# A fused Perceiver layer: late matmuls ahead of the fourth transposes, the time-step projection in the products' second bank, and the joining of blocks in three steps

## The chip, the cores and the metric

The kernel runs on one NeuronCore of one Trainium2 chip. The metric is the device time of one execution in microseconds (us), and a time is the median of several executions. A profile is one execution, recorded by the hardware profiler. The engines are PE (TensorE, matrix products; its weight loads are listed as PEld), DVE (VectorE), ACT (ScalarE), POOL (GpSimd) and SP (SyncE, which issues most transfers). Each engine works through its own queue in program order, and waits where an operand or a buffer is not ready.

## The reference

The layer has three parts, each added to a residual stream `x` of 16 sequences with 128 rows of 512 numbers, all in fp32. First comes cross-attention, 16 heads of 32, over a context of 2048 rows per sequence. Then a state-space (Mamba) block with 1024 channels and 16 states, followed by an MLP with norms. The last part is a small mixture of experts. What matters here is the first two:

```python
def _L0_xattn_ref(queries, context, wq, bq, wk, bk, wv, bv, wo, bo):
    q = queries @ wq.T + bq
    k = context @ wk.T + bk
    v = context @ wv.T + bv
    ...
    attn = jnp.einsum('bhnd,bhsd->bhns', q, k) * scale
    attn = jax.nn.softmax(attn, axis=-1)
    out = jnp.einsum('bhns,bhsd->bhnd', attn, v)
    ...
    return out @ wo.T + bo

def _mamba(Z, in_proj_w, conv_w, conv_b, x_proj_w, dt_proj_w, dt_proj_b, A_log, D, out_proj_w):
    xz = jnp.einsum('bld,ed->ble', Z, in_proj_w)
    x, z = jnp.split(xz, 2, axis=-1)
    x = jax.nn.silu(_causal_dw_conv(x, conv_w, conv_b))
    x_dbl = jnp.einsum('bld,ed->ble', x, x_proj_w)
    dt, Bm, Cm = jnp.split(x_dbl, [DTR, DTR + DS], axis=-1)
    dt = jax.nn.softplus(jnp.einsum('blr,dr->bld', dt, dt_proj_w) + dt_proj_b)
    ...
    y = ys.transpose(1, 0, 2) + x * D
    y = y * jax.nn.silu(z)
    return jnp.einsum('bld,ed->ble', y, out_proj_w)
```

## The kernel before, in words

**Steps.** One loop (L1152) runs over 314 steps `u`. In the first 256, a step does one block of attention: one sequence `b`, one quarter `sb` of its context (512 rows), one group `hg` of four heads. So 4 steps make a quarter and 16 a sequence. Work of other stages is hung into the same steps: each step reads what the dictionaries `loads`, `middle`, `late`, `after` and `inner` hold for it (L1058 to L1112). The order is written out by hand; no scheduler moves anything. What is called `late` is matmul work of other stages: the normalized inputs turned (`turned`) and projected to queries (`queries`), the rescaling of a sequence's four quarters (`scaled`, twice in each of two steps), the output projection (`attended`), the transposes for the state-space block (`z_turned`), its input projections (`x_part`, `z_part`), `x_proj`, the time-step projection (`dt_first`) and the output projection (`projected`).

**A step of attention**, in the order of TensorE's queue: `scores` (L299) of four heads into the four PSUM banks `banks[0..3]`; `weighted` (L343), which is the product with `v` of the step before, into `avp`; `x_products` (L237), two products for the next context block, into `pa` and `pc`; four `turn`s (L330), each of which transposes a quarter of the exponentials into one bank; the late matmuls, in banks 0, 1, 2 of the step; and `y_products` (L237). In odd steps the last is one product into `pa`, in even steps two, into `pc` and `pa`.

**Who empties the banks.** VectorE takes the row maxima of the scores (L307), ScalarE the exponentials (L317). The transposes of turns 0, 1 and 3 are copied out by ScalarE (L335), those of turn 2 by VectorE (L333). Late results are read by ScalarE or VectorE, as the stage needs. A bank's next writer on TensorE waits until it has been read.

**Joining.** Each quarter has its own row maxima. When a sequence is done, `joined` (L418 to L424, VectorE) gathers them and takes their differences to the common one, `shares` (L428, ScalarE) takes exponentials, and `joined_last` (L433 to L436, VectorE) makes the factors that `scaled` applies. They stand in the steps `e`, `e + 1` and `e + 1` after the sequence's last, `e` being a multiple of 16.

**The state-space block** lags behind, for two sequences at a time (a group, 32 steps). Per step, `decays` (L653, ScalarE) and `scan` (L667, L670, VectorE) are done twice, with the products before on GpSimd (L632) and the sums after (L683). `dt_first` (L599 to L608) is a small matmul, read from its bank by ScalarE (Abs, L603) and VectorE (L606). It is due at `s - 3 + 4 * ec`, which leaves 3 when divided by 4. The gate silu(z) is `silu_first` (L551 to L553, three ScalarE operations, in `after`), `silu_second` (L558, VectorE, at the step's end) and `silu_third` (L562, L563, ScalarE and GpSimd, in the next step). `Z_GATES` holds the steps, counted from the group's start, at which the eight channel blocks are due.

**After step 255** the attention's banks serve the MLP and the experts, whose matmuls are fed into the remaining 58 steps of the scan.

Of the kernel before, what the change touches and what calls it, by code (L numbers as in the profile page):

```python
# [34 lines left out]
def perceiver_layer(ctx: ExitStack, tc: tile.TileContext, a: dict, out: bass.AP):  # L35
# [68 lines left out]
    NG = B // GB  # L104
    NU = B * SB * 4
    LAG = 22
    Z_GATES = (20, 22, 23, 24, 25, 36, 38, 40)
    NF = B // MB
    with ExitStack() as es:
        acon = es.enter_context(tc.tile_pool(name="acon", bufs=1))  # L110
# [18 lines left out]
        pc = psum.tile([P, 2, 256], FP, tag="pc", name="pc")  # L129
# [11 lines left out]
        def heads(ps):  # L141
            return ps.rearrange("p (k q) -> p k q", q=P)
# [137 lines left out]
        def x_sums(of, g, ph, pa, pc):  # L280
            sums[of](g, ph, ph, pc, held[of])
# [41 lines left out]
                )  # L323
            prs[u] = pr

        def turn(u, i):

            ps = heads(banks[i])
            for j in range(4):
                nc.tensor.transpose(ps[:, j, :], prs[u][:, j, i * P : (i + 1) * P], ident)  # L330
            pT = pool.tile([P, 4, P], FP, tag="pT", name="pT", bufs=4)
            if i == 2:
                nc.vector.tensor_copy(pT, ps)  # L333
            else:
                nc.scalar.copy(pT, ps)  # L335
            pts[u, i] = pT
# [76 lines left out]
        def joined(b):  # L413

            parts, sm = stats[b]
            nm = keep.tile([P, SB, H], FP, tag="nm", name=f"nm{b}")
            for j in range(4):
                nc.vector.tensor_copy(  # L418
                    nm.rearrange("p s (k j) -> p s k j", j=4)[:, :, :, j], parts[j]
                )  # L420
            lo = keep.tile([P, 1, H], FP, tag="lo", name="lo")
            flat = lo.rearrange("p a h -> p (a h)")
            nc.vector.tensor_reduce(flat, nm.rearrange("p s h -> p h s"), AX.X, ALU.min)
            nc.vector.tensor_tensor(nm, lo.to_broadcast([P, SB, H]), nm, ALU.subtract)  # L424
            stats[b] = nm, sm, lo, flat

        def shares(b):
            nc.scalar.activation(stats[b][0], stats[b][0], AF.Exp)  # L428

        def joined_last(b):  # L430
            nm, sm, lo, flat = stats[b]
            stats[b] = nm
            nc.vector.tensor_tensor(sm, sm, nm, ALU.mult)  # L433
            nc.vector.tensor_reduce(flat, sm.rearrange("p s h -> p h s"), AX.X, ALU.add)
            nc.vector.reciprocal(lo, lo)
            nc.vector.tensor_tensor(nm, nm, lo.to_broadcast([P, SB, H]), ALU.mult)  # L436

        fxs = {}
# [300 lines left out]
        def load_wex():  # L739
            fcs["wex"] = fpool[0].tile([P, KC, D], FP, tag="wex", name="wex")  # L740
            nc.sync.dma_start(fcs["wex"], a["wex"])
# [313 lines left out]
            units[-1][1].extend([call(experts, m, i), call(gated, m, (i,)), call(result, m, i)])  # L1055


        late, after, inner, middle, loads = ({} for _ in range(5))  # L1058

        def put(where, u, f):  # L1060
            where.setdefault(u, []).append(f)

        for b in range(B):
            s = 16 * b
            if b:
                put(loads, s - 8, lambda b=b: load_x(b))
                put(loads, s - 5, lambda b=b: load_w(0, b))
                put(inner, s - 7, lambda b=b: moments_of(b))
                put(middle, s - 6, lambda b=b: root_of(b))
                put(inner, s - 6, lambda b=b: normal(b))  # L1070
                put(late, s - 5, lambda ps, b=b: turned(b, ps))
                put(late, s - 4, lambda ps, b=b: queries(b, ps))
            e = s + 16
            put(loads, e + 5, lambda b=b: load_w(3, b))
            put(inner, e, lambda b=b: joined(b))
            put(middle, e + 1, lambda b=b: shares(b))
            put(inner, e + 1, lambda b=b: joined_last(b))
            for sb in range(SB):
                put(inner, e + 2 + sb // 2, lambda b=b, sb=sb: spread_out(b, sb))
                put(late, e + 3 + sb // 2, lambda ps, b=b, sb=sb: scaled(b, sb, ps))  # L1080
            put(late, e + 6, lambda ps, b=b: attended(b, ps))
            put(middle, e + 7, lambda b=b: root_of(b))
            put(inner, e + 7, lambda b=b: normed(b))
            put(late, e + 8, lambda ps, b=b: z_turned(b, ps))
        for g in range(NG):
            p = 32 * (g + 1)
            for ec in range(EC):
                put(loads, p + 8 + ec, lambda g=g, ec=ec: load_win(g, ec))
                put(loads, p + 8 + ec, lambda g=g, ec=ec: load_win(g, EC + ec))
                put(late, p + 9 + ec, lambda ps, g=g, ec=ec: x_part(g, ec, ps))  # L1090
                put(late, p + 9 + ec, lambda ps, g=g, ec=ec: z_part(g, ec, ps))
                put(after, p + 10 + ec, lambda g=g, ec=ec: silu_first(g, ec, xas))
                put(after, p + Z_GATES[ec], lambda g=g, ec=ec: silu_first(g, ec, zss))
            put(late, p + 18, lambda ps, g=g: x_proj(g, ps))
            s = p + LAG
            for ec in range(EC):
                put(loads, s - 4 + 4 * ec, lambda ec=ec: load_dtproj(ec))
                put(late, s - 3 + 4 * ec, lambda ps, g=g, ec=ec: dt_first(g, ec, ps))
                put(middle, s - 2 + 4 * ec, lambda g=g, ec=ec: dt_second(g, ec))
                put(inner, s - 2 + 4 * ec, lambda g=g, ec=ec: dt_third(g, ec))  # L1100
            for i in range(GB):
                for ec in range(WS):
                    put(loads, s + 32 + 2 * i, lambda g=g, i=i, ec=ec: load_wout(g, i, ec))
                put(loads, s + 31 + 2 * i, lambda b=g * GB + i: reload_x(b))
                put(late, s + 33 + 2 * i, lambda ps, g=g, i=i: projected(g, i, ps))
# [32 lines left out]
        ps = banks[2]  # L1138
# [13 lines left out]
        for u in range(last):  # L1152
            live = u < NU
            g, r = divmod(u - 32 - LAG, 32)
            scans = 0 <= g < NG

            made, phase = divmod(u + 3, 4)
            makes = 0 < made < B * SB
            of, phase = ("k", "v")[phase // 2], phase % 2
            load_bc(u + 2 - 32 - LAG, 0)  # L1160
            if u % 4 == 1 and made + 1 < B * SB:
                load_ctx(made + 1, ("c00", "c10", "c11"))
            if u % 4 == 2 and made + 1 < B * SB:
                load_ctx(made + 1, ("c01",))
            for f in loads.get(u, ()):
                f()
            if scans:
                decays(g, r, 0)
            if u > NU:
                while fed < feeds * (u - NU) // (last - 1 - NU):  # L1170
                    feed(fed)
                    fed += 1
            load_bc(u + 1 - 32 - LAG, DS)
            if u == NU + 1:
                load_rows()
            if live:
                scores(u)
            if 1 <= u <= NU:
                weighted(u - 1)
            if u == NU:  # L1180
                att.close()
                open_ffn()
            if u == NU + 8:
                load_wex()
            if live:
                maxima(u)
            if makes:
                x_products(of, made, phase, pa, pc)
            if live:
                exps(u)  # L1190
            if makes and u % 4 == 1:
                ctx_sums(made, ("t1", "t2"))
            if 0 <= u + 1 - 32 - LAG < 32 * NG:
                inputs(*divmod(u + 1 - 32 - LAG, 32))
            if makes and u % 4 == 1:
                ctx_sums(made, ("t3", "t4"))
            silu_third()
            if scans:
                scan(g, r, 0)
            if makes:  # L1200
                hold(of, made, pa, "u1")
            if scans:
                decays(g, r, 1)
            if makes:
                x_sums(of, made, phase, pa, pc)
            if live:
                for i in range(4):
                    turn(u, i)
            if scans:
                scan(g, r, 1)  # L1210
            for f in middle.get(u, ()):
                f()
            for i, f in enumerate(late.get(u, ())):
                f(banks[i % 4 if live else 2 + i % 2])
            for f in after.get(u, ()):
                f()
            for f in inner.get(u, ()):
                f()
            if makes:
                y_products(of, made, phase, pa, pc)  # L1220
                y_sums(of, made, phase, pa, pc)
            silu_second()
# [76 lines left out]
```

## Time and profile before

| what | value |
|---|---|
| three runs | 3925.76, 3926.09 and 3930.98 us, median 3926.09 |
| the profiled execution | 3930.69 us, its span 3928.9 us |
| instructions in the span | 70620 |
| mean granted TensorE clock | 0.986 |
| a period of 32 steps, 2002.45 to 2404.50 us | 402.05 us: PE busy 396.5, DVE 315.0, ACT 281.8, POOL 255.8 |
| the tail, 3185 to 3880 us | 695 us: PE busy 646.0, DVE 431.1, ACT 296.9, POOL 377.5 |

The span runs from the first to the last instruction of the profiled execution. Busy time is the time in which an engine had an instruction in hand, and a matmul that waits for its bank while the one before it drains is counted in it. In a row of the timeline stand the start in us, the duration in us, the engine, the line of the kernel, the operation, what it writes and reads, the shape, and how many such instructions were merged; in square brackets, where the engine sat idle before it, for how long and who released it. A row of the view of waits gives who waited, for whom, the total in us, how often, and the longest.

### The profile page before, as it was taken

What the parts mean: (1) busy time and instruction counts of PE and PEld (TensorE: products, weight loads), DVE (VectorE), ACT (ScalarE), POOL (GpSimd) and SP (SyncE); (2) the same over time, 40 slices, a digit from 0 to 9 for tenths busy, and PEclk for the clock granted to TensorE, in tenths of its full rate; (3) what the DMA queues carried; (4) which work ended last, traced back from release to release, by engine and by line L of the source; (5) the groups of instructions that cost most, each with busy time, mean ns of one, the idle gap of its engine ahead of it and who ended that gap; (6) DMA issues with size and microseconds to landing.
All of it is one profiled execution on the core that took longest, in us unless ns stands there. A gap on an engine that the chain in (4) does not pass through costs nothing.

```text
span 3928.9 us, 70620 instructions
## 1 busy us (share of the span) xinstructions
PE 3791.6 (97%) x26120; PEld 2877.2 (73%) x26120; DVE 2736.4 (70%) x4900; ACT 2416.6 (62%) x5799; POOL 2102.8 (54%) x1968
## 2 busy tenths in 40 slices
PE   7999999999999999999999999999999989989998
PEld 6878787778777877787778777877777756555654
DVE  3444445887778777877787778777877777767732
ACT  2555556777677766776677767776777664444421
POOL 1111213675667566756566657656765675657710
PEclk9999999999999999999999999999999989999999
DMA  2111122444444444443544353535453567567641
GB/s 90 41 33 47 53 64 86 137 146 135 139 154 147 138 137 157 138 151 125 163 140 150 116 173 125 164 114 171 130 159 110 167 237 236 179 229 262 223 159 59
DMA packets 341224, 548.41 MB, mean 140 GB/s; under 512 B 24432, under 2 KB 225408, under 8 KB 340624
## 3 DMA queue, kind: packets, MB, share of 16 engines
q1 hardware_dynamic: 340464, 543.28, 42.6%
q8 instruction: 206, 3.38, 0.4%
q14 instruction: 138, 1.13, 0.1%
q0 software_dynamic: 416, 0.63, 0.1%
HBM read 527.29 MB, written 16.52 MB: 138 GB/s over the span
## 4 chain that ended last, share of the span: by engine, by line
PE 72%; DVE 16%; ACT 6%; issue 3%; DMA 2%; POOL 1%; SPq 0%; DVEq 0%; ACTq 0%; POOLq 0%
PE pa L237 18%; PE pc L237 13%; PE bank L330 8%; PE bank L299 7%; PE bank L515 6%; PE avp L343 5%; DVE hst L667 4%; DVE nm L307 4%; DVE w L670 2%; ACT hst L653 2%; PE bank L696 2%; PE bank L395 2%; PE bank L461 2%; PE bank L856 2%; PE bank L826 1%
## 5 line engine op out<-in xcount | busy, mean ns | idle before, releaser
L307 DVE TENSOR_REDUCE nm<-bank 128x1 f32<-128x512 f32 x1024 | 635.2, 682 | 253.6 <-PE bank L299 253.0
L683 POOL TENSOR_TENSOR ysum<-ysum,w 128x512 f32<-128x512 f32 x384 | 500.2, 1303 | 550.4 <-DVE hst L646 328.1
L317 ACT ACTIVATE pr<-bank,nm 128x512 f32<-128x512 f32 x1024 | 689.8, 687 | 108.1 <-DVE nm L307 102.7
L632 POOL TENSOR_TENSOR w<-dx,bc 128x512 f32<-128x512 f32 x512 | 646.5, 1284 | 3.8
L667 DVE TENSOR_TENSOR_SCAN hst<-hst,w 128x512 f32<-128x512 f32 x456 | 556.7, 1221 | 2.0 <-ACT hst L653 1.8
L653 ACT ACTIVATE hst<-dt,alog 128x254 f32<-128x254 f32 x912 | 437.1, 479 | 163.7 <-DVE hst L646 143.0
L330 PE MATMUL bank<-ident,pr 128*128 128x128 f32 x4096 | 496.1, 274 | 10.5 <-ACT pr L317 10.4
L330 PEld LDWEIGHTS bank<-ident,pr 128*128 128x128 f32 x4096 | 464.9, 142 | 42.6 <-ACT pr L317 16.4
L335 ACT COPY pT<-bank 128x512 f32<-128x512 f32 x768 | 401.7, 585 | 63.1 <-PE bank L330 63.1
L343 PEld LDWEIGHTS avp<-pT,v 128*32 128x32 f32 x8192 | 208.1, 110 | 201.5 <-issue 194.6
L670 DVE TENSOR_TENSOR w<-hst,bc 128x512 f32<-128x512 f32 x456 | 315.1, 691 | 46.9 <-DMA bc<-bcd 31.6
L299 PE MATMUL bank<-kt,qT 32*128 32x512 f32 x2048 | 310.6, 643 | 11.4 <-DVE dt L606 7.9
L229 POOL TENSOR_TENSOR t<-c,c 128x512 f32<-128x512 f32 x128 | 164.8, 1288 | 251.7 <-PE pc L237 244.1
L343 PE MATMUL avp<-pT,v 128*32 128x128 f32 x8192 | 278.6, 276 | 5.3 <-DVE v L267 5.3
L237 PE MATMUL pa<-t,ks 128*128 128x256 f32 x1024 | 249.8, 387 | 0.0
L333 DVE COPY pT<-bank 128x512 f32<-128x512 f32 x256 | 176.8, 691 | 101.1 <-PE bank L330 99.6
L237 PE MATMUL pa<-vs,t 128*128 128x256 f32 x1008 | 244.7, 386 | 0.0
L515 PE MATMUL bank<-zT,win 128*128 128x256 f32 x1024 | 235.6, 383 | 7.6 <-ACT hs L840 4.6
L515 PEld LDWEIGHTS bank<-zT,win 128*128 128x128 f32 x1024 | 191.4, 191 | 39.6 <-ACT pT L335 8.0
L237 PEld LDWEIGHTS pa<-t,ks 128*128 128x128 f32 x1024 | 187.0, 191 | 36.5 <-issue 11.8
L237 PEld LDWEIGHTS pa<-vs,t 128*128 128x128 f32 x1008 | 185.5, 190 | 34.8 <-issue 12.3
L317 ACT ACTIVATION_READ_ACCUMULATOR pr<-bank,nm 128x1 f32 x1024 | 209.9, 205 | 0.0
(270 smaller groups left out, 6850.2 us busy)
## 6 DMA issues: line engine op xcount, KB each, us to landing
bc<-bcd SPq DMA_DIRECT2D x512, 512.0 KB, 4.4
c<-in_ctxT_dram SPq DMA_DIRECT2D x256, 256.0 KB, 4.4
wf<-in_w_dram SPq DMA_DIRECT2D x128, 512.0 KB, 7.2
wqo<-in_wqkvo_dram SPq DMA_DIRECT2D x128, 256.0 KB, 4.9
win<-in_win_dram SPq DMA_DIRECT2D x128, 256.0 KB, 4.7
wout<-in_wout_dram SPq DMA_DIRECT2D x128, 256.0 KB, 4.2
x<-in_x_dram SPq DMA_DIRECT2D x16, 256.0 KB, 4.2
x1d<-x SPq DMA_DIRECT2D x16, 256.0 KB, 2.1
```

Of the source, the lines that this page charges most:

```text
L237: nc.tensor.matmul(ps[:, r, :], l[:, kc, r * P : (r + 1) * P], m[:, kc, :], start=(i in (1, 2, 5) and r == 0 and kc == 0), stop=(r == 1 an ...
L299: nc.tensor.matmul(banks[j], qts[b][rows, hg, :], kts[u // 4, hg][rows, :], start=True, stop=True)
L307: nc.vector.tensor_reduce(stats[b][0][j][:, sb, hg : hg + 1], banks[j], AX.X, ALU.max, negate=True)
L317: nc.scalar.activation(pr[:, j, :], banks[j], AF.Exp, bias=nm[j][:, sb, hg : hg + 1], accum_out=sm[:, sb, h : h + 1],)
L330: nc.tensor.transpose(ps[:, j, :], prs[u][:, j, i * P : (i + 1) * P], ident)
L335: nc.scalar.copy(pT, ps)
L343: nc.tensor.matmul(avp[j * HD : (j + 1) * HD, hg, :], vts[u // 4, hg // 2, i // 2][:, i % 2, hg % 2 * P + j * HD : hg % 2 * P + (j + 1) * HD],
L515: nc.tensor.matmul(ps, w[:, kc, :], zTs[g][:, kc, :], start=(kc == 0), stop=(kc == KC - 1))
L632: nc.gpsimd.tensor_tensor(w, dx.unsqueeze(1).to_broadcast([P, NH // 2, GT]), bcs[g * 32 + r, 0][:, i * NH // 2 : (i + 1) * NH // 2, :], AL ...
L653: nc.scalar.activation(bt(h[:, k, :])[:, :, 1:], bt(dt)[:, :, 1:], AF.Exp, scale=aneg[:, ec, n : n + 1],)
L667: nc.vector.tensor_tensor_scan(flat, flat, w.rearrange("p n t -> p (n t)"), 0.0, ALU.mult, ALU.add)
L683: nc.gpsimd.tensor_tensor(s, s, w, ALU.add)
```

## The change

Five things change. The first late matmul of a step in which attention runs goes into bank 3, before the fourth transposes, and further late ones into banks 0 and 1; the fourth turn (`turn(u, 3, ...)`) follows them, in the bank after theirs. Where a step has no late work, the turns stay as they were. The time-step projection leaves `late` for a new list `behind`, which is issued after the fourth turn; it goes into `pc` while context products are made, and into bank 2 later. The joining is spread over `inner` of step `e - 1` (`joined`), `middle` of `e` (`shares`), and a new list `head`, read ahead of the row maxima, in `e + 1` (`joined_second`) and `e + 2` (`joined_third`). In the first three steps of each sequence, turn 2 is copied by ScalarE too. And five of the eight entries of `Z_GATES` change.

```diff
-    Z_GATES = (20, 22, 23, 24, 25, 36, 38, 40)
+    Z_GATES = (20, 22, 25, 34, 36, 38, 40, 50)
...
-        def turn(u, i):
-
-            ps = heads(banks[i])
+        def turn(u, i, bank):
+
+            ps = heads(banks[bank])
...
-            if i == 2:
+            if i == 2 and u % 16 > 2:
                 nc.vector.tensor_copy(pT, ps)
...
-        def joined_last(b):
+        def joined_second(b):
             nm, sm, lo, flat = stats[b]
-            stats[b] = nm
             nc.vector.tensor_tensor(sm, sm, nm, ALU.mult)
             nc.vector.tensor_reduce(flat, sm.rearrange("p s h -> p h s"), AX.X, ALU.add)
             nc.vector.reciprocal(lo, lo)
+
+        def joined_third(b):
+            nm, sm, lo, flat = stats[b]
+            stats[b] = nm
             nc.vector.tensor_tensor(nm, nm, lo.to_broadcast([P, SB, H]), ALU.mult)
...
-            put(inner, e, lambda b=b: joined(b))
-            put(middle, e + 1, lambda b=b: shares(b))
-            put(inner, e + 1, lambda b=b: joined_last(b))
+            put(inner, e - 1, lambda b=b: joined(b))
+            put(middle, e, lambda b=b: shares(b))
+            put(head, e + 1, lambda b=b: joined_second(b))
+            put(head, e + 2, lambda b=b: joined_third(b))
...
-                put(late, s - 3 + 4 * ec, lambda ps, g=g, ec=ec: dt_first(g, ec, ps))
+                put(behind, s - 3 + 4 * ec, lambda ps, g=g, ec=ec: dt_first(g, ec, ps))
...
+            for f in head.get(u, ()):
+                f()
             if live:
                 maxima(u)
...
+            after_turns = late.get(u, ())
             if live:
-                for i in range(4):
-                    turn(u, i)
+                for i in range(3 if after_turns else 4):
+                    turn(u, i, i)
             if scans:
                 scan(g, r, 1)
             for f in middle.get(u, ()):
                 f()
-            for i, f in enumerate(late.get(u, ())):
-                f(banks[i % 4 if live else 2 + i % 2])
+            for i, f in enumerate(after_turns):
+                f(banks[(3 + i) % 4 if live else 2 + i % 2])
+            if live and after_turns:
+                turn(u, 3, (3 + len(after_turns)) % 4)
+            for f in behind.get(u, ()):
+                f(pc.rearrange("p k q -> p (k q)") if makes else banks[2])
             for f in after.get(u, ()):
                 f()
```

More of the change, by code (lines that the diff above doesn't have):

```diff
@@ L1055, in perceiver_layer @@
             units[-1][1].extend([call(experts, m, i), call(gated, m, (i,)), call(result, m, i)])
-        late, after, inner, middle, loads = ({} for _ in range(5))
+        late, after, inner, middle, loads, head, behind = ({} for _ in range(7))
         def put(where, u, f):
```

## The prediction

> **What bounds the kernel now.** I read the page first: busy shares, then the chain that ended last.
>
> ```profile
> PE 3791.6 (97%) x26120; PEld 2877.2 (73%) x26120; DVE 2736.4 (70%) x4900; ACT 2416.6 (62%) x5799; POOL 2102.8 (54%) x1968
> PE 72%; DVE 16%; ACT 6%; issue 3%; DMA 2%; POOL 1%; SPq 0%; DVEq 0%; ACTq 0%; POOLq 0%
> ```
>
> TensorE is the bound, and no edit removes one of its instructions. So the change is worth the stalls that it takes from TensorE or gives to it. Next, who ended TensorE's idle time between 600 and 3150 us, where attention and scan run together:
>
> ```profile
> PE bank L299 <- DVE dt L606: 7.9, 14, 0.6
> PE bank L569 <- ACT pT L335: 7.3, 6, 1.2
> PE bank L508 <- ACT pT L335: 5.8, 7, 0.9
> PE avp L343 <- DVE v L267: 5.3, 6, 0.9
> ```
>
> These are the three places of the diff: the time-step projection, late matmuls after the turns (L330), the joining before `v`. But idle time shows half of it: a row that waits inside is counted busy. So I took starts, in the timeline of TensorE:
>
> ```profile
> 2014.73 1.91 PE L330 MATMUL bank<-ident,pr 128*128 128x128 f32 x16
> 2016.48 1.11 PE L448 MATMUL bank<-ident,fx 128*128 128x128 f32 x8
> 2017.42 0.60 PE L599 MATMUL bank<-xd,dtw 128*128 128x256 f32 x2
> 2017.85 1.89 PE L237 MATMUL pa<-vs,t 128*128 128x256 f32 x8
> 2019.67 2.10 PE L299 MATMUL bank<-kt,qT 32*128 32x512 f32 x8
> 2021.70 1.08 PE L343 MATMUL avp<-pT,v 128*32 128x128 f32 x32
> ...
> 2096.67 1.91 PE L330 MATMUL bank<-ident,pr 128*128 128x128 f32 x16
> 2098.71 1.56 PE L515 MATMUL bank<-zT,win 128*128 128x256 f32 x6
> ```
>
> From start to next start, the turns take 1.75 us before L448 but 2.04 before L515: 0.29 waited. The scores (L299) take 2.03 at 2019.67; undisturbed they take 1.07 (2009.09 to 2010.16). Done for every step, this repeats every 32 steps (402.05 us). Steps below are modulo 32. Stalls per 32 steps, in us:
>
> - **Bank 0 after the turns**, late matmul waits for ScalarE's copy of turn 0: steps 6, 10, 12, 14, 16, 22 about 0.41 each (0.1 of it a slow restart), 2.46; step 18 (L569) 1.62; step 24 (L508) 1.44; steps 4, 8, 20, 28 together 0.49. Sum 6.0.
> - **Scores behind late evacuations on VectorE**: 0.63 at 7 and at 31 (`dt`, L606), 0.49 + 0.39 at 27 and 28, 0.96 at 4 and at 20 (two products of `scaled`, then `dt`), 0.10 at 11 and 15. Sum 4.15.
> - **Joining**: 1.09 at step 1 (`weighted` waits for `v`), 0.55 at step 2. Sum 1.64.
>
> That is 11.8 of 402 us. Before step 54 there is next to none.
>
> **The change, part by part.** *Late work in bank 3, then turn 3.* The late matmul no longer waits for a copy. Turn 3 waits in its place, but later by the length of the late work. Copy 0 ends 1.6 to 2.0 us after the turns start (in the step at 1976.38: turns 1982.02, three copies from 1983.17, 0.585 each). Three turns are 1.31, late work 0.44 to 6.9, so turn 3 comes at 1.75 or more: mostly free, 0.05 with the shortest. Step 18: `x_proj` can start at once; its last operand leaves GpSimd at 2210.13, its last matmul would come near 2212.4. Step 24: copy 0 is late there because step 23 issues a gate (L558, 1.49 on VectorE), and row maxima start 2.65 us into the step, not 1.16. The gates of 23 and 24 go to 34 and later, so that cause goes too. SyncE's issues (`x1d`, `xnd`, `bcd`) keep their order and only start earlier. Left of 6.0: 0.25. **Gain 5.75.**
>
> What it adds: turn 3's copy now stands on ScalarE behind the late evacuations, ahead of `dt`'s Abs and Exp, the gate and the y sums, and the next scores wait for it in bank 0, 1 or 2. With ScalarE free it lands 0.9 us after turn 3 (0.2 to start, 0.585, a semaphore). TensorE has 1.82 us of products before the scores in odd steps, 3.55 in even ones. So it is hidden where ScalarE is less than 0.9 late. At 11 and 15 `dt` and gate now end the queue; I place the next step's exponentials about 0.5 later than now. They start at 2.70 us in a step, and turns at 5.64 have about 0.3 to spare. Zero, and half a us at both if that cover is gone.
>
> *Time-step projection in `pc`.* It is issued where u mod 4 = 3, when the y product writes only `pa`. `pc` was read by then (`v`, 1972.01 to 1972.70; turns end at 1973.49) and is next written 3.9 us into the following step. So `dt` drops from the scores' path: 7, 31, 27 and 28 go to nothing. At 4 and 20 the second `scaled` product stays: its VectorE row ends at 2020.19, TensorE is ready at 2019.67; I leave 0.6 of 0.96. The gates new in 2 and 18 put one more ScalarE row (0.43) into 3 and 19: 0.1 together. **Gain 4.15 − 1.2 − 0.1 = 2.85.** The price if `pc` were not free: one wait for `v`, below 0.7.
>
> *Joining in three steps.* VectorE at the join, now:
>
> ```profile
> 1986.46 2.02 DVE L418 COPY nm<-nm 128x16 f32<-128x16 f32 x4
> 1988.52 0.27 DVE L423 TENSOR_REDUCE lo<-nm 128x16 f32<-128x64 f32 x1
> 1988.82 0.44 DVE L424 TENSOR_TENSOR nm<-lo,nm 128x64 f32<-128x64 f32 x1
> 1989.18 0.68 DVE L267 TENSOR_TENSOR v<-pc,u2vu 128x512 f32<-128x512 f32 x1
> 1989.78 2.47 DVE L307 TENSOR_REDUCE nm<-bank 128x1 f32<-128x512 f32 x4
> ```
>
> Moved to the end of step 15 or 31, it no longer delays `v`; the second and third parts (0.63 + 0.27 + 0.25, then 0.73) go ahead of row maxima, where VectorE waits 1.2 us for scores anyway. That takes away 1.64. But in step 31 it lands ahead of step 0's maxima. `dt` ends 10.2 us into step 31, the next step starts at 9.64 (10.28 less 0.63), maxima are due at 10.8. The trace has two prices for the block: 2.8 us here and 1.13 at 2190.19. The four copies differ (1246, 169, 712, 170 ns against 236 and 170): GpSimd was busy from 1986.23. The Trainium skill (SBUF — State Buffer, Who interferes with whom) speaks against this place: a VectorE copy in a two-port mode and a GpSimd instruction lock each other out for a whole instruction. GpSimd starts a sum of 1.27 us at 1975.95, right where the block will begin. By the rule alone, each of four copies could wait 1.27: over 5 us, exponentials 4 us late. By the row it is 1.13 to 2.8: joined by 11.4 to 13.05, exponentials at 2.5 to 4.1 into step 0, against 3.0 bearable: 0 to 1.05 of stall. I take 0.6, nearer the contended row. Step 16 follows a longer step and waits for nothing. **Gain 1.64 − 0.6 = 1.04.** Turn 2 on ScalarE in steps 0 to 2 (0.585 for 0.691): four copies end near 9.1, scores at 9.2 or later; nothing.
>
> *Gates moved.* Each is three ScalarE rows of 0.42, one on VectorE, then one more of each on ScalarE and GpSimd in the next step; their number stays. In 2 and 18 they end before TensorE's y products do (10.4 against 10.9 us into the step): nothing beyond the 0.1 above. If that cover failed, up to 0.4 each.
>
> *Tail.* With no attention, `dt` always takes bank 2, behind `x_part` at 267 and 271 and `projected` at 279. By the L530 rows after the transition (2.2 us past the matmuls' end) I charge 3 us in all; 0 to 6.
>
> **Sum.** 5.75 + 2.85 + 1.04 = 9.65 per 32 steps; five whole periods 48.2, the last to step 252 about 8.9, steps 54 to 63 about 3.2: 60. Less 3: **57 us**. The profiled execution took 3930.7 around its span of 3928.9, which gives 3874; the median, 3926.1, gives 3869. I say **3872**.
>
> **Rivals.**
> 1. *Half of it comes back.* The joining costs 1.05, and the fuller ScalarE queue pushes exponentials past their cover at 0, 8, 12, 16, 24 and 28 by 0.5 to 0.8: 4.5 of 9.65 per period is lost. For it: exponentials have only 0.3 to spare, and the avs copy precedes them in every fourth step. Against: ScalarE is busy 282 of 402 us. Gives about **3900**.
> 2. *Slower: turn 3's copy becomes the wait.* The place is the scores after odd steps with late work, nine per 32. If the copy lands later than 1.8 us after turn 3, the rest is stall; at 2.9 (1.07 each) the gain is gone. At 3.4, 14.4 less 9.65 is 4.8 per period: about **3957**. For it: a gate's three rows and `dt`'s two are 2.2 us on that engine. Against: they are issued behind the copy, and ScalarE shows idle time before the y sums (0.72 us at 1975.86).
> 3. *No change*: both meet, **3926**.
>
> **How the numbers follow.** Forecast 0.71 (own range 3858 to 3886), first rival 0.18, slower 0.07, no change 0.04. Measurements of this kernel tell about 0.2% (8 us) from nothing. Range: all stalls gone (−72, no tail price) is 3854; the first rival's side reaches to 3903. Faster 0.89, same 0.04, slower 0.07.
>
> **What would show it.** TensorE's wait on `dt` by L299 gone between 600 and 3100 us; L569 and L508 starting 1.31 us after the turns; L343 no longer waiting on `v` at step 1. A period near 392.4 us, not 402.05. Wrong: L299 waiting on ScalarE's `pT` in odd steps (second rival), or the turns waiting on `pr` by over 1 us in many steps (first).

## The result and the profile after

| | before | changed |
|---|---|---|
| runs, us | 3925.76, 3926.09, 3927.45, 3930.98 | 3880.22, 3883.60, 3884.85, 3886.99 |
| median, us | 3926.77 | 3884.22 |
| profiled execution (span), us | 3930.69 (3928.9) | 3884.85 (3883.1) |
| first scores begin, us | 58.86 | 57.87 |
| first scores to step 255 | 3109.92 | 3059.95 |
| of it, a period of 32 steps | 401.97 | 393.77 |
| tail, from step 255 to the end | 760.1 | 765.3 |

The ratio to before is 0.9889, with a 95% interval of 0.9872 to 0.9906: 42.6 us less, where 54 (3926.1 less 3872) had been said. Between the two profiled executions it is 45.8: the part with attention won 51.0, and the tail gave 5.1 back. The page of the changed kernel, busy shares and the chain that ended last:

```profile
PE 3771.4 (97%) x26120; PEld 2868.8 (74%) x26120; DVE 2713.3 (70%) x4852; ACT 2445.5 (63%) x5847; POOL 2104.8 (54%) x1968
PE 81%; DVE 10%; ACT 4%; issue 2%; DMA 2%; POOL 1%; SPq 0%; DVEq 0%; ACTq 0%; POOLq 0%
```

The busy share of PE reads 97% in both: of the 45.8 us that went, 20.2 had been counted as busy (3791.6 less 3771.4), so they fell out of both sides of the fraction. The chain tells more. VectorE and ScalarE held 22% of it and now hold 14%.

Who ended TensorE's idle time between 600 and 3150 us, in the changed kernel (who waited, for whom, total us, how often, longest):

```profile
PE bank L330 <- ACT pr L317: 12.4, 19, 6.4
PE avp L829 <- DMA wf<-in_w_dram: 6.0, 1, 6.0
PE bank L299 <- DVE avs L458: 5.7, 12, 0.5
PE bank L330 <- ACT pT L335: 2.0, 7, 0.3
PE pc L237 <- DVE kt L257: 0.2, 1, 0.2
```

All four waits of before that the prediction showed are gone: `dt`, the two on `pT` ahead of late matmuls, and `v`. The 6.4 of the first row (in step 254) and the L829 row (in the tail's first 20 us) belong to the change from attention to tail, where the kernel before waits too. What remains in the periods is turns that wait for exponentials, scores that wait for `scaled`, and turn 3 that waits for `pT`.

TensorE's timeline of the changed kernel, step 3 and then step 10:

```profile
1986.64 1.47 PE L330 MATMUL bank<-ident,pr 128*128 128x128 f32 x12
1987.95 1.06 PE L451 MATMUL bank<-ident,fx 128*128 128x128 f32 x8
1988.85 0.60 PE L330 MATMUL bank<-ident,pr 128*128 128x128 f32 x4
1989.28 0.60 PE L602 MATMUL pc<-xd,dtw 128*128 128x256 f32 x2
1989.72 1.89 PE L237 MATMUL pa<-vs,t 128*128 128x256 f32 x8
1992.08 1.14 PE L299 MATMUL bank<-kt,qT 32*128 32x512 f32 x8 [0.47 <-DVE avs L458]
...
2067.44 1.47 PE L330 MATMUL bank<-ident,pr 128*128 128x128 f32 x12
2068.75 3.62 PE L518 MATMUL bank<-zT,win 128*128 128x256 f32 x16
2072.20 0.60 PE L330 MATMUL bank<-ident,pr 128*128 128x128 f32 x4
```

Three turns, late work, the fourth turn, then `dt` into `pc`. From the turns to L518 it is 1.31 us, which is three turns with nothing waited, and turn 3 follows without a wait as well. The scores after step 3 still stand 0.47 behind `scaled`.

Waits inside busy rows don't show in the idle time, so lengths of steps, from start of scores to next start, are the measure from here on. They are read in one period of each profile, steps 160 to 191; over steps 64 to 223 the periods of the changed kernel differ by less than 0.02 us. These steps differ by over 0.1 us (all modulo 32):

| step | before | changed | | step | before | changed |
|---|---|---|---|---|---|---|
| 0 | 10.935 | 11.947 | | 10 | 14.781 | 14.391 |
| 1 | 10.299 | 9.208 | | 12 | 18.406 | 17.965 |
| 2 | 11.473 | 10.935 | | 14 | 14.779 | 14.391 |
| 3, 19 | 10.58 | 11.08 | | 16 | 14.832 | 14.564 |
| 4, 20 | 12.96 | 11.96 | | 18 | 16.015 | 14.682 |
| 6, 22 | 14.76 | 14.37 | | 24 | 12.814 | 11.465 |
| 7, 31 | 10.28 | 9.64 | | 27 | 10.564 | 10.077 |
| 8 | 11.465 | 11.868 | | 28 | 15.030 | 14.901 |

Together that is 8.20 us per period where 9.65 had been said. Two questions are left. Which of the parts earned what, and what are the 1.0 us more in step 0 and the 0.4 more in step 8?

### The profile page after: what moved, and what is told of

It is laid out like the page before. It is cut to its first block, busy times and chain, and to the rows that moved or that the text cites. A ratio compares the mean times of both kernels' runs of the same rounds, so it can differ in the third digit from the quotient of the medians.

```text
span 3883.1 us, 70354 instructions
## 1 busy us (share of the span) xinstructions
PE 3771.4 (97%) x26120; PEld 2868.8 (74%) x26120; DVE 2713.3 (70%) x4852; ACT 2445.5 (63%) x5847; POOL 2104.8 (54%) x1968
## 3 DMA queue, kind: packets, MB, share of 16 engines
q1 hardware_dynamic: 340464, 543.28, 42.6%
## 4 chain that ended last, share of the span: by engine, by line
PE 81%; DVE 10%; ACT 4%; issue 2%; DMA 2%; POOL 1%; SPq 0%; DVEq 0%; ACTq 0%; POOLq 0%
PE pa L237 21%; PE pc L237 15%; PE bank L330 10%; PE bank L299 7%; PE bank L518 6%; PE avp L343 6%; PE bank L699 3%; DVE hst L670 2%; DVE nm L307 2%; PE bank L859 2%; DVE w L673 2%; PE bank L395 2%; PE bank L464 2%; PE bank L960 1%; PE bank L829 1%
## 5 line engine op out<-in xcount | busy, mean ns | idle before, releaser
L335 ACT COPY pT<-bank 128x512 f32<-128x512 f32 x816 | 437.6, 585 | 222.0 <-PE bank L330 217.9
L330 PE MATMUL bank<-ident,pr 128*128 128x128 f32 x4096 | 525.4, 275 | 16.2 <-ACT pr L317 14.3
L299 PE MATMUL bank<-kt,qT 32*128 32x512 f32 x2048 | 297.7, 642 | 6.1 <-DVE avs L458 5.7
L518 PE MATMUL bank<-zT,win 128*128 128x256 f32 x1024 | 234.6, 383 | 4.6 <-ACT hs L843 4.6
L518 PEld LDWEIGHTS bank<-zT,win 128*128 128x128 f32 x1024 | 192.0, 192 | 30.9 <-ACT hs L843 5.0
L333 DVE COPY pT<-bank 128x512 f32<-128x512 f32 x208 | 143.8, 691 | 89.1 <-PE bank L330 86.5
```

The source lines that it names most:

```text
L299: nc.tensor.matmul(banks[j], qts[b][rows, hg, :], kts[u // 4, hg][rows, :], start=True, stop=True)
L518: nc.tensor.matmul(ps, w[:, kc, :], zTs[g][:, kc, :], start=(kc == 0), stop=(kc == KC - 1))
```

## Experiments

The first four each take one part alone, or put one part back; they ran once each on the same chip, where one run of the kernel before took 3934.65, so they are compared by their periods and not by their times. Then come the places that had stayed short of the forecast, together on another chip (kernel before: median of seven runs 3928.13, 3923.58 to 3934.22), and repeats on a third.

### Late work ahead of turn 3, alone

```diff
-                for i in range(4):
-                    turn(u, i)
+                for i in range(3 if late.get(u) else 4):
+                    turn(u, i, i)
...
-                f(banks[i % 4 if live else 2 + i % 2])
+                f(banks[(3 + i) % 4 if live else 2 + i % 2])
+            if live and late.get(u):
+                turn(u, 3, (3 + len(late[u])) % 4)
```

This is the kernel before with the first part only: gates, joining and time-step projection are the old ones.

> The kernel before with one part of the change alone: late matmuls in bank 3 ahead of the fourth turn. Joining, time-step projection and gates stay as before. My theory: the waits for the copy of turn 0 go at steps 6, 10, 12, 14, 16, 18 and 22 (about 3.9 us per 32 steps), but step 24 stays near 12.8 us, since the gates of steps 23 and 24 are still there and turn 3 now waits for the same late copy. The time-step projection still holds a bank, now the last one, so that steps 7 and 31 keep some of their 0.63 us. A period of about 397.5 us against 402.0, the time about 27 us below before. Rival: the order alone frees step 24 (11.5 us), and a period is near 396.2 us.

Measured: 3902.39 us, a period of 397.26, so 4.71 of the 8.20. Steps 6, 10, 12, 14, 16, 18 and 22 took what they take in the changed kernel or up to 0.17 less. Step 24 came to 12.38 only: the old gates still hold it.

Steps 7 and 31 fell to 9.64, as if `dt` no longer stood in the scores' way, though it was still a late matmul. It does stand there. TensorE's timeline of this kernel, from step 31 into step 0:

```profile
1957.49 0.60 PE L599 MATMUL bank<-xd,dtw 128*128 128x256 f32 x2
1957.92 0.60 PE L330 MATMUL bank<-ident,pr 128*128 128x128 f32 x4
1958.36 1.89 PE L237 MATMUL pa<-vs,t 128*128 128x256 f32 x8
1960.18 1.76 PE L299 MATMUL bank<-kt,qT 32*128 32x512 f32 x8
1961.87 1.08 PE L343 MATMUL avp<-pT,v 128*32 128x128 f32 x32
```

`dt` is now in bank 3, the last that the scores write. Their first matmul starts on time, and their last ones wait: 1.69 us to the next row instead of 1.07. The 0.62 has only moved into step 0 (11.55), and likewise from 7 into 8 (12.09). Steps 31 and 0 together took 21.20 against 21.22 before, 7 and 8 together 21.73 against 21.75. A step's length by starts books a wait where it is found, so neighbours must be read as pairs.

### The gates back

```diff
-    Z_GATES = (20, 22, 25, 34, 36, 38, 40, 50)
+    Z_GATES = (20, 22, 23, 24, 25, 36, 38, 40)
```

> The changed kernel with the old list of gates. My theory: step 24 goes from 11.46 us back to about 12.8, nothing else in the period moves by more than 0.3, so a period is near 395.1 us against 393.77; the tail after step 255 comes back by about 2 us. Time about 6 us above the changed kernel. Rival: the gates play no part, step 24 stays at 11.5 and the period at 393.8 us.

Measured: 3889.05 us, a period of 395.16. Only step 24 moved, from 11.465 to 12.861; the new gates in 2 and 18 cost nothing that can be seen. (By place, six of the eight entries differ; what matters is that steps 23 and 24 have lost their gates, and 34 and 50, which are 2 and 18 modulo 32, have got one.) TensorE's timeline of this kernel in step 24:

```profile
2259.20 1.81 PE L330 MATMUL bank<-ident,pr 128*128 128x128 f32 x12
2260.84 0.60 PE L511 MATMUL bank<-ident,x 128*128 128x128 f32 x4
2262.37 0.66 PE L330 MATMUL bank<-ident,pr 128*128 128x128 f32 x4 [0.94 <-ACT pT L335]
```

The late matmul got ahead of the wait, and turn 3 inherited it: late work of 0.44 us is too little to lie behind. Without the new gates the order gains nothing in step 24 here, and 0.43 in the first experiment. In step 24 these two differ in one row of VectorE ahead of the maxima, the norm's last (L502, L499 there), which took 1.19 us here and 0.71 there. The new gates without the new order were not run.

### The old joining

```diff
-            if i == 2 and u % 16 > 2:
+            if i == 2:
...
-            put(inner, e - 1, lambda b=b: joined(b))
-            put(middle, e, lambda b=b: shares(b))
-            put(head, e + 1, lambda b=b: joined_second(b))
-            put(head, e + 2, lambda b=b: joined_third(b))
+            put(inner, e, lambda b=b: joined(b))
+            put(middle, e + 1, lambda b=b: shares(b))
+            put(inner, e + 1, lambda b=b: joined_second(b))
+            put(inner, e + 1, lambda b=b: joined_third(b))
```

> The changed kernel with the joining where it was before, and turn 2 always copied by VectorE. My theory: the 1.01 us that step 0 gained come from the joining ahead of its row maxima, so step 0 falls from 11.95 to 10.94 us, while steps 1 and 2 rise to about 10.3 and 11.4 us: a period near 394.3 us against 393.77, time 3 to 4 us above the changed kernel. Rival: step 0 is late for another reason, such as the projection or turn 2 on ScalarE, and stays at 11.9 us; then the period is near 395.3 us, time about 9 us above.

Measured: 3884.02 us, a period of 394.25. Step 0 went back to 10.935, steps 1 and 2 to 10.30 and 11.50, step 16 to 14.39. The new joining is worth 0.48 per period: 1.66 won in 1 and 2, and 1.19 lost in 0 and 16. The total did not show even that, since the tail was 2.9 us shorter here.

### The time-step projection back among the late matmuls

```diff
-                put(behind, s - 3 + 4 * ec, lambda ps, g=g, ec=ec: dt_first(g, ec, ps))
+                put(late, s - 3 + 4 * ec, lambda ps, g=g, ec=ec: dt_first(g, ec, ps))
```

> The changed kernel with the time-step projection back among the late matmuls, so in one of the four banks. My theory: steps 7 and 31 wait again (up to 0.6 us each) and 27 to 28 by about 0.4 more, while step 8 gives back its 0.40 and the tail comes back by 2 us or more: a period of 394.5 to 395.2 us against 393.77, time 3 to 6 us above the changed kernel. Rival: the stall at the projection was only a place where VectorE's queue caught up, and what goes at 7, 27 and 31 comes back at 8, 28 and 0: a period within 0.3 us of 393.77.

Measured: 3894.26 us, a period of 395.46, a little above what was expected, so `pc` is worth 1.69. TensorE's timeline of this kernel, the scores after step 7 and those after step 27:

```profile
2039.39 0.60 PE L602 MATMUL bank<-xd,dtw 128*128 128x256 f32 x2
2039.83 0.60 PE L330 MATMUL bank<-ident,pr 128*128 128x128 f32 x4
2040.26 1.89 PE L237 MATMUL pa<-vs,t 128*128 128x256 f32 x8
2042.09 1.76 PE L299 MATMUL bank<-kt,qT 32*128 32x512 f32 x8
...
2301.01 0.61 PE L602 MATMUL bank<-xd,dtw 128*128 128x256 f32 x2
2301.45 0.60 PE L330 MATMUL bank<-ident,pr 128*128 128x128 f32 x4
2301.89 1.89 PE L237 MATMUL pa<-vs,t 128*128 128x256 f32 x8
2304.50 1.14 PE L299 MATMUL bank<-kt,qT 32*128 32x512 f32 x8 [0.72 <-DVE dt L609]
```

Alone in bank 3, `dt` hides its wait inside the scores of 8 and 0; as the second late matmul, in bank 0 (step 27), it holds their start. For step 8 I had expected less time and saw 0.22 more, because the 0.62 is found there. In step 0 the 0.62 costs nothing at all (11.944 against 11.947): its turns wait for exponentials anyway, by 0.62 less when the scores come 0.62 late. So the new joining eats what `pc` won at step 31. The rest is 0.41 for the pair 27 and 28 and 0.39 each in 4, 18 and 20, less 0.17 in 16.

### Gathering on GpSimd: what step 0 waits for

VectorE and GpSimd at the start of step 0 in the changed kernel, which begins at 2342.68, and TensorE's turns:

```profile
2342.79 0.48 DVE L609 TENSOR_SCALAR dt<-pc,dtb 128x256 f32<-128x256 f32 x1
2342.82 0.06 DVE L649 MEMSET hst<- 128x4 f32 x1
2342.89 1.27 POOL L686 TENSOR_TENSOR ysum<-ysum,w 128x512 f32<-128x512 f32 x1 [2.98 <-DVE hst L649]
2343.18 1.45 DVE L418 COPY nm<-nm 128x16 f32<-128x16 f32 x4
...
2344.50 2.50 POOL L635 TENSOR_TENSOR w<-dx,bc 128x512 f32<-128x512 f32 x2
2344.67 0.26 DVE L423 TENSOR_REDUCE lo<-nm 128x16 f32<-128x64 f32 x1
...
2344.97 0.88 DVE L424 TENSOR_TENSOR nm<-lo,nm 128x64 f32<-128x64 f32 x1
2345.77 2.47 DVE L307 TENSOR_REDUCE nm<-bank 128x1 f32<-128x512 f32 x4
...
2348.32 0.67 PE L330 MATMUL bank<-ident,pr 128*128 128x128 f32 x3
...
2349.32 1.64 PE L330 MATMUL bank<-ident,pr 128*128 128x128 f32 x13 [0.34 <-ACT pr L317]
```

The joining is the price: 2.6 us stand between `dt` and the maxima, which start 3.1 us into the step. Of that, 1.45 are four copies of 128x16 numbers, beside a GpSimd sum that began just ahead of them. The turns then run after their exponentials, 2.66 us in place of 1.75, and the product after them is 0.10 slow to start. To test it, the four copies moved to GpSimd, and the reduction and difference behind the maxima.

```diff
-                nc.vector.tensor_copy(
+                nc.gpsimd.tensor_copy(
...
+        def joined_rest(b):
+            nm, sm = stats[b]
...
+            put(past, e, lambda b=b: joined_rest(b))
...
                 maxima(u)
+            for f in past.get(u, ()):
+                f()
```

> The changed kernel with the four small copies of the joining on GpSimd, and its reduction and difference on VectorE behind the row maxima of the next step. My theory: the 1.01 us in step 0 are VectorE's joining ahead of the maxima, so step 0 falls from 11.95 to about 10.94 us and nothing else in the period rises by over 0.2: a period near 392.8 us against 393.77, time about 6 us below the changed kernel. Rival: the joining only moves on, behind the maxima it delays the scan, the second decays and the four copies, and step 1 or 2 takes the 1 us back; the period stays at 393.7 us.

Measured: 3873.73 us, a period of 392.97. Step 0 took 11.32, not the 10.94 expected, and step 16 went back to 14.39 though turn 2 was still on ScalarE there, so the turn had not cost it. Nor had the copies by themselves: in the experiment before this one they stood on VectorE, took 2.5 us at the end of step 15, and step 16 took 14.39 all the same. In the changed kernel the difference (L424) and the product behind it (L561, `silu_second`) took 0.89 and 1.51 us beside GpSimd products, and the maxima started 2.53 us into step 16; with the projection back they took 0.23 and 0.42, and the maxima started at 1.77. The rest of step 0, in this kernel's timeline (step 0 begins at 2339.3):

```profile
2341.68 2.49 POOL L639 TENSOR_TENSOR w<-dx,bc 128x512 f32<-128x512 f32 x2
...
2342.87 0.25 DVE L427 TENSOR_REDUCE lo<-nm 128x16 f32<-128x64 f32 x1
2343.15 1.10 DVE L428 TENSOR_TENSOR nm<-lo,nm 128x64 f32<-128x64 f32 x1
2344.17 1.22 DVE L674 TENSOR_TENSOR_SCAN hst<-hst,w 128x512 f32<-128x512 f32 x1
...
2344.95 1.91 PE L330 MATMUL bank<-ident,pr 128*128 128x128 f32 x16
...
2346.23 0.69 DVE L267 TENSOR_TENSOR v<-pc,u1v 128x512 f32<-128x512 f32 x1
...
2346.98 0.48 PE L237 MATMUL pc<-vs,c 128*128 128x256 f32 x1
```

The turns are on time now. But the reduction and the difference stand ahead of the scan, and the difference (L428) took 1.10 us beside GpSimd; so the scan, and after it `v`, came later, and the product that writes `pc` waited for `v` to have read it: 2.03 us from the turns instead of 1.74, and 0.10 of slow start.

### The second scan behind the late evacuations

Steps 3, 19 and 27 keep a wait at their scores. VectorE reads the late bank (`scaled`, or the turned inputs L387) only after the second scan, which stands ahead of it in its queue.

```diff
-            if scans:
+            late_scan = u % 16 == 3 or u % 32 == 27
+            if scans and not late_scan:
                 scan(g, r, 1)
...
                 turn(u, 3, (3 + len(after_turns)) % 4)
+            if scans and late_scan:
+                scan(g, r, 1)
```

> The changed kernel with the second scan of steps 3, 19 (scaled) and 27 (turned) behind the late evacuations in VectorE's queue. My theory: the 0.50 us left at 3 and at 19, and the 0.39 at 28, are VectorE reading the late banks only after that scan; with the order turned, steps 3 and 19 fall from 11.08 to about 10.58 us, 28 from 14.90 to 14.51: a period near 392.4 us against 393.77, time about 8 us below. Rival: the scan that now ends 1.4 us later delays the next step's first decays and exponentials, so that steps 4, 20 and 28 rise by as much: a period at 393.7 us or above.

Measured: 3872.23 us, a period of 392.27. Steps 3 and 19 fell by 0.54 to 10.54, step 28 by 0.39 to 14.51. TensorE's timeline of this kernel, step 3 to the next scores:

```profile
1985.31 0.60 PE L330 MATMUL bank<-ident,pr 128*128 128x128 f32 x4
1985.74 0.60 PE L602 MATMUL pc<-xd,dtw 128*128 128x256 f32 x2
1986.18 1.89 PE L237 MATMUL pa<-vs,t 128*128 128x256 f32 x8
1988.00 1.14 PE L299 MATMUL bank<-kt,qT 32*128 32x512 f32 x8
```

The 0.47 before L299 is gone. It was the order of VectorE's own queue.

### The tail as it was

```diff
+    Z_LAST = (20, 22, 23, 24, 25, 36, 38, 40)
...
+            if b < B - 1:
...
+            else:
+                put(inner, e, lambda b=b: joined(b))
...
-                put(after, p + Z_GATES[ec], lambda g=g, ec=ec: silu_first(g, ec, zss))
+                put(after, p + (Z_GATES if g < NG - 1 else Z_LAST)[ec], lambda g=g, ec=ec: silu_first(g, ec, zss))
...
-                put(behind, s - 3 + 4 * ec, lambda ps, g=g, ec=ec: dt_first(g, ec, ps))
+                put(behind if s - 3 + 4 * ec < NU - 1 else late, s - 3 + 4 * ec, lambda ps, g=g, ec=ec: dt_first(g, ec, ps))
```

Gates of the last group, joining of the last sequence, and `dt` from step 255 on are again those of before.

> The changed kernel, in which only what falls behind step 255 is as before: the old gates for the last group, the old joining for the last sequence, the time-step projection among the late matmuls from step 255 on. The period must stay at 393.77 us. My theory: the changed kernel's tail of 765.3 us (760.1 before) is made by gates and joining in the tail itself (each alone gave back 3 to 3.6), so it falls to 760 to 762 us, time about 4 us below the changed kernel. Rival: what counts are the gates of the group before (its last one came from step 264 to 274), which this kernel keeps, or the earlier end of attention; the tail stays above 764 us.

Measured: 3879.78 us, a period of 393.75, a tail of 759.4 against 765.3. That seems to confirm it; but the two experiments before this one kept the new gates and the projection in bank 2 in the tail, and theirs were 759.6 and 760.5. They did not leave the tail quite alone either: the last sequence's joining was changed in the one, and the second scan of five steps after 255 in the other.

### Together

Gathering on GpSimd, the scan behind, the tail as it was, and turn 2 always on VectorE.

> The changed kernel with the last three edits together, and turn 2 always copied by VectorE. My theory: they act on different steps and add up: steps 0, 3, 19, 28 as said for each, step 16 from 14.56 to 14.39 us, a period near 391.2 us, the tail near 761 us; time 3862 to 3868 us. Rival: VectorE's queue, fuller at the joins with turn 2 back, gives half of it back: a period of 392.5 us or more, time about 3874 us.

Measured: median of four runs 3867.58 us (3864.32 to 3868.26), a ratio of 0.9843 to before (0.9827 to 0.986), and a period of 391.50. The gains add: 0.80 and 1.49 were measured apart, 2.27 together. This version beats both kernels.

### Repeats

Both kernels unchanged, for the tail: the changed one twice, that of before once.

> The changed kernel once more, unedited, to see how one kernel's profile varies. The live part to step 255 must be the same within 0.1 us per period (393.77 us). Theory: the tail's 5.1 us over before belong to the change, so the tail is again 764 to 766 us. Rival: the tail varies by several us from one execution to the next, as the runs of one kernel do (3880.2 to 3887.0), and this one falls elsewhere between 759 and 766 us.

> The same again. Theory and rival as for the one before: a tail of 764 to 766 us, or a tail anywhere between 759 and 766 us.

> The kernel before once more, unedited. A period of 401.97 us. Theory: the tail is again 759 to 761 us. Rival: it varies by itself, and falls 2 us or more from the 760.1 of the first profile.

| | time | period | first scores to step 255 | tail |
|---|---|---|---|---|
| changed, profile of the result | 3884.85 | 393.77 | 3059.95 | 765.3 |
| changed, first repeat | 3885.00 | 393.75 | 3059.84 | 765.4 |
| changed, second repeat | 3883.43 | 393.75 | 3059.38 | 762.9 |
| before, profile of the result | 3930.69 | 401.97 | 3109.92 | 760.1 |
| before, repeat | 3927.88 | 401.97 | 3110.54 | 758.5 |

The part with attention repeats itself; the tail of one and the same kernel moves by up to 2.5 us, so that the second repeat fell outside the 764 to 766 expected. The changed kernel's tail is longer by 2.8 to 6.9. Waits in the open do not make that: TensorE's idle time in the tail is 69.1, 72.3 and 69.2 us in the three profiles of the changed kernel, 69.5 and 67.5 in the two of before. The rest lies in busy rows. The granted clock is one candidate: its mean over the tail was 0.944, 0.946 and 0.945 in the changed kernel, 0.947 and 0.950 before. If busy rows stretch as the clock falls, 0.003 of some 690 us would be 2 us; that is an estimate, and no run here isolates it.

## Why the prediction was right, and where it was off

**The bound and the method held.** The bound was TensorE's stalls, counted from starts; all four waits named went away, and the changed kernel had the 57 us sum's sign and most of its size. The median, 3884.2, lies in the forecast's own range (3858 to 3886), but at its far end, 12 us above the 3872 and 16 below the first rival's 3900. Per period 8.20 came of 9.65, by the profiles. Put back one at a time, gates, joining and `dt` were worth 1.39, 0.48 and 1.69, and the late order alone 4.71; that is 8.27, near the whole, though single steps share their waits (0, 8 and 24).

**Late work and gates, 5.75 said.** Six steps with 2.46 gave 2.44 in the run with that part alone. Step 18 gave 1.33 of 1.62: `x_proj` itself takes 3.60 us from start to next start in both kernels, so only 1.48 stood outside it, and the changed kernel still loses 0.09 before it and 0.06 in a slow start behind it. Step 24 gave 1.35 of 1.44, and the cause was named rightly: with the old gates the order gained 0.43 there in one kernel and nothing in the other. What was mis-sized is step 8: "0.05 with the shortest" was 0.40. The changed kernel there, step 8 beginning at 2037.27:

```profile
2038.51 0.55 DVE L502 TENSOR_SCALAR x<-x,mv,rstd 128x512 f32<-128x512 f32 x1
...
2038.97 2.48 DVE L307 TENSOR_REDUCE nm<-bank 128x1 f32<-128x512 f32 x4
...
2043.54 0.99 ACT L656 ACTIVATE hst<-dt,alog 128x254 f32<-128x254 f32 x2 [0.31 <-DVE hst L649]
...
2044.46 1.06 ACT L335 COPY pT<-bank 128x512 f32<-128x512 f32 x2
...
2045.09 0.66 PE L330 MATMUL bank<-ident,pr 128*128 128x128 f32 x4 [0.28 <-ACT pT L335]
```

Step 7 is 0.63 shorter, but VectorE's rows for `dt` and the norm are not, so the maxima start 1.70 us into step 8 instead of 1.16. The scan, the decays and the copies follow one another from there. Copy 0 begins 7.19 us into the step where it had been 6.79, and ends 2.1 us after the turns start, past the 1.6 to 2.0 that I took from another step. Turn 3 has only 0.44 us of late work to lie behind. Of the 0.63 won in 7, 0.40 comes back in 8. The kernel before, where step 8 begins at 2066.89:

```profile
2068.05 2.48 DVE L307 TENSOR_REDUCE nm<-bank 128x1 f32<-128x512 f32 x4
...
2073.68 1.54 ACT L335 COPY pT<-bank 128x512 f32<-128x512 f32 x3
```

This is read from the timelines; no run moved VectorE's rows out of step 8.

**Time-step projection, 2.85 said.** `pc` was free, as read, and 7 and 31 lost their 0.64 each. Pairs 3 and 4, and 19 and 20, won 0.50 each, with 0.5 left at the scores (0.6 said). The miss is "7, 31, 27 and 28 go to nothing": 0.39 stayed at 28, since the turned inputs (L387) are read by VectorE behind the second scan whether `dt` is there or not. The experiment with the scan behind removed just that. I had booked the whole wait on `dt`, the last of two reads.

**Joining, 1.04 said.** The wait for `v` went (1.09 and 0.54). Step 0 lost 1.01 where I took 0.6, at the upper end of 0 to 1.05. The block itself fell into its bracket of 1.13 to 2.8, at the contended end: 2.6 us. Between two prices, one beside a running GpSimd sum and one without, I had seen the sum begin where the block would be, and still took a value between. Step 16, said to wait for nothing, lost 0.17. Whole part: 0.48.

These terms are the shortfall: step 0 0.41, step 8 0.40, step 18 0.29, steps 27 and 28 0.26, step 16 0.14, together 1.50 of 1.45. Over the run: 41.1 for five periods (48.2 said), 7.1 for the last (8.9), 1.8 for steps 54 to 63 (3.2), and 1.0 because the first scores came earlier, which differs between runs of one kernel by up to 1.8 and so is luck.

**The tail, 3 said, 0 to 6.** It was 5.1 between the profiles. Whether gates and `dt` in bank 2 cause it stays open: putting them back gave 759.4, and leaving them while the steps before were shortened gave 759.6 and 760.5. These lie 4.8 to 5.9 below the changed kernel's first tail, more than the 2.5 that one kernel shows between runs; but all three ran on another chip than the changed kernel's repeats, with a mean granted clock of 0.947 to 0.952 in the tail, so neither chip nor clock is ruled out.

**Rivals.** That turn 3's copy becomes the wait at the scores is refuted for the part with attention: among TensorE's waits of the changed kernel no row has L299 waiting for `pT`. Nor does a wait hide inside the scores: from start to next start they take 1.07 us in every step of a period but 28, whose 1.46 went when the scan was moved behind. The first rival named two mechanisms: its joining price of 1.05 came true almost exactly; late exponentials at 8, 12, 16, 24 and 28 did not, save 0.17 at 16, which came from the joining, and at 8 the three turns run on time (1.31 by starts) and it is copy 0 that is late.

## What to carry to other kernels

Price a moved block by the trace row whose neighbours it will have, not by a mean of its rows. When a step is made shorter, ask which engine does not get shorter with it: here VectorE's leftovers gave back 0.40 of 0.63 one step later, and its queue order was then worth 1.49 per period, nearly as much as the projection's new bank. When a wait goes from one step, add up the neighbouring steps, since another bank can hide the same wait in the next row.

## What was not expected of the hardware

A VectorE instruction on very few numbers can take until the GpSimd instruction beside it has ended. The difference of 128x64 numbers (L424; L428 in the gathering experiment) took 0.22 to 0.23 us in every joining where no GpSimd instruction ran beside it. In step 0 of the changed kernel it took 0.88 and ended at 2345.85, 0.08 after the first of the two GpSimd products begun at 2344.50. In the gathering experiment it took 1.10 and ended at 2344.25, again 0.08 after both products were through (2344.17). In all twelve joinings between 600 and 3100 us it ended 0.08 to 0.09 us after a GpSimd instruction, in both kernels: 886 ns on average in the changed kernel, 385 before, where less of the GpSimd instruction was left. The reduction just ahead of it (L423) took 0.26 beside the same product, so not every VectorE instruction waits.

Of the four copies in step 0, two waited: they took 1.02, 0.17, 0.38 and 0.17 us, the first and the third ending 0.04 after a GpSimd instruction, the second and the fourth running beside the next one. By the strict reading that the prediction made of the Trainium skill's rule (SBUF — State Buffer, Who interferes with whom), that the later of two such instructions waits for the whole of the other, each of the four could have waited 1.27. Such waits lie inside the busy time, and no view of waits lists them.
